# PSUM banks from a written list instead of from a pool, in a two-layer graph transformer

## The chip, the cores and the metric

One core of one Trainium2 chip runs the whole program in one launch. The metric is device time in microseconds (us); smaller is better. A core has five engines with a queue each: TensorE (PE in the profile, with its weight loads as PEld), VectorE (DVE), ScalarE (ACT), GpSimd (POOL) and SyncE (SP, which here only issues DMAs). Engines meet through semaphores: an instruction can wait until a counter that another engine raises has reached a value.

## The reference

32 graphs of 512 nodes with 256 features go through two attention layers. Everything is float32.

```python
x = _layernorm(x + _L0_gnn_ref(x, adj, ...), axis=-1)     # layer 0
x = _layernorm(x + _L1_gnn_ref(x, adj, ...), axis=-1)     # layer 1

def _L0_gnn_ref(x, adj, ...):            # 8 heads of 32
    allowed = (adj > 0) | (jnp.swapaxes(adj, 1, 2) > 0) | eye
    q, k, v = split(x @ Wqkv.T + bqkv)
    attn = softmax(where(allowed, q @ k.T / sqrt(32), -inf))
    x = _layernorm(x + (attn @ v) @ Wo.T + bo) * g1 + b1
    ff = relu(x @ W1.T + b1) @ W2.T + b2               # 256 -> 1024 -> 256
    return _layernorm(x + ff) * g2 + b2

def _L1_gnn_ref(x, adjacency, ...):      # no feed-forward part
    scores = where(adjacency == 0, -inf, q @ k.T / sqrt(32))
    return (softmax(scores) @ v) @ Wo.T + bo
```

So for each graph there are two attentions, one feed-forward block and four row normalisations (numbered 1 to 4 in the kernel: 1 after the first attention, 2 after the feed-forward part, 3 at the end of layer 0, 4 at the end of layer 1).

## The kernel before

The kernel keeps one graph's data in on-chip memory and is written as small steps, methods of a class `Graph`; one object stands for one of the 32 graphs. The order of the steps is written out by hand: `opening` starts the first graphs, `period(a, b, c, d, e)` (L1484) is called 26 times and moves five neighbouring graphs on by one stage each, and `closing` ends the last ones. In one `period`, graph `b` is in its second attention, graph `c` goes from the end of its first attention through its feed-forward block to the start of its second attention, and graph `d` starts its first attention. Each engine executes its own instructions strictly in the order in which the steps are listed.

PSUM, where TensorE writes its results, has eight banks[...]. Four banks hold the attention scores of one step (`s`), one holds the accumulated product of probabilities and values (`acc`), and the other three are the pool `ps_d` (L156), from which all other results of TensorE come: the dense products (`psQK`, `psV`, `psO`, `psH`, `psF`), the transpositions (`psT`), the row sums of the probabilities (`psR`) and some biases at the start (`psB`). Every such result is one tile, asked for in `bank` (L186). 1158 of them are made in the run. A bank that is used again makes the first matmul of the new tile wait until the last reader of the old tile in that bank is done, and until the old tile's own matmuls are.

The steps that matter below, with what they issue:

- `project(layer, h)` (L507): the output projection, psO, two blocks of 256 columns; read by DVE in `add(n, i)` (L515), n = 1 in layer 0 and 4 in layer 1, two adds for each psO tile (h = 0: i = 0 and 1; h = 1: i = 2 and 3).
- `transpose(n, h)` (L353): psT, four 128x128 transpositions; copied to SBUF by ACT in `transpose_out` (L363, L364).
- `hidden(h, f)` (L559): psH, two blocks of the hidden layer; read by ACT in `relu` (L567, L569). `mlp(i)` (L571) is the second product, psF, and `add(2, i)` reads it on DVE.
- `query_key(layer, which, c, h)` (L377): psQK; copied with its bias by ACT in `query_key_out` (L384, L388).
- `value(layer, h)` (L367): psV; copied by ACT in `value_out` (L374, L375).
- `scores` (L391), `exp` (L406, ACT, 2048 elements a row), `masked` (L409, DVE, L411), `product` (L413, L418) and `fold` (L433, DVE, L434) are the attention itself. They use no bank of `ps_d`.
- `sums` (L436, L442) is psR, read by DVE in `blocks` (L477, L483).
- `root` (L530, POOL), `offset` (L536, DVE, L538) and `norm` (L553, ACT, L554) normalise rows; `center` and `affine` (L542, L548, DVE) do so with gain and bias.

Dense products run through a helper, `dense` (L159), so all their matmuls have the line L162; the tile's name tells them apart. With `wide` off, a product is cut into four pieces of 32 output partitions that run side by side in TensorE.

Two places of `period` carry the prediction. The first is this one, graph `c` entering its feed-forward block (L1583 to L1603, other steps left out):

```python
c.add(1, 3)                      # DVE, reads psO
c.transpose(1, 0)                # PE
d.value(0, 1, wide=True)         # PE
c.transpose_out(1, 0)            # ACT
c.hidden(0, 4, wide=True)        # PE
c.hidden(0, 2, wide=True)        # PE
```

The second is graph `c` entering its second attention while `b` leaves it (L1737 to L1763):

```python
b.add(4, 2); c.query_key(1, 0, 0, 0); b.add(4, 1)
c.query_key_out(1, 0, 0, 0)      # ACT
d.product(0, 4); b.add(4, 3); d.product(0, 5)
c.value(1, 0)                    # PE
c.norm(3, 2); c.transpose(2, 1); b.add(4, 0)
c.query_key(1, 1, 0, 0, wide=True)
```

Of the kernel before, what the change touches and what calls it, by code (L numbers as in the profile page):

```python
# [9 lines left out]
F32 = mybir.dt.float32  # L10
# [17 lines left out]
def kernel(ctx: ExitStack, tc: tile.TileContext, t: dict, out: bass.AP):  # L28
# [15 lines left out]
    P = 128  # L44
# [106 lines left out]
    def plain(pools: ExitStack):  # L151
# [4 lines left out]
        ps_d = pools.enter_context(tc.tile_pool(name="ps_d", bufs=3, space=PSUM))  # L156
        hbm = pools.enter_context(tc.tile_pool(name="hbm", bufs=2, space=bass.MemoryType.DRAM))

        def dense(out, lhsT, rhs, start, stop, wide):  # L159
# [3 lines left out]

        SPREAD = {(0, 0), (1, 0)}

        SMALL = {"y", "z", "cent", "sT", "total", "r", "st", "part"} | {
            f"{t}{n}" for t in ("mv", "rs", "ms") for n in range(1, 5)
        }

        class Graph:  # L170
# [6 lines left out]
            def at(self, tag, n, shape, dtype=F32, **kw):  # L177

                key = (tag, n)
                if key not in self.tiles:  # L180
                    name = f"{tag}_{self.b}" + "".join(f"_{i}" for i in (n if isinstance(n, tuple) else () if n is None else (n,)))
                    pool = small if tag in SMALL else ps_s if tag == "s" else ps_a if tag == "acc" else work
                    self.tiles[key] = pool.tile([P, *shape], dtype, tag=tag, name=name, **kw)
                return self.tiles[key]

            def bank(self, kind, n, shape):  # L186

                key = (kind, n)
                if key not in self.tiles:
                    name = f"ps{kind}_{self.b}" + "".join(f"_{i}" for i in n)  # L190
                    self.tiles[key] = ps_d.tile([P, *shape], F32, tag="d", name=name)
                return self.tiles[key]

            def final(self, layer):
# [2497 lines left out]
    with ExitStack() as pools:  # L2692
        plain(pools)
# [207 lines left out]
```

## Time and profile before

| | us |
|---|---|
| median of 3 runs | 3055.63 |
| the 3 runs | 3054.47 to 3057.43 |
| the profiled execution, its device time | 3058.88 |
| its span, first to last instruction | 3057.1 |
| TensorE busy in the span | 2976.1 |
| VectorE busy | 2706.1 |
| ScalarE busy | 1746.1 |
| GpSimd busy | 921.5 |
| largest group on TensorE: scores, L398, 8192 passes | 573.6 |
| largest group on VectorE: masking, L411, 512 instructions of 2.278 us | 1162.4 |
| largest group on ScalarE: exp, L407, 512 instructions of 1.880 us | 962.8 |

The profile is one execution of the program. A matmul in it is a pipelined instruction: each stays in the record for 380 ns (256 columns) or 596 ns (512 columns), while the next one starts long before that; the end is modelled. A float32 product appears as two passes, a transposition as one. "Idle before" is the time for which an engine did nothing ahead of an instruction, with the engine and instruction that ended it, and gaps under 150 ns are not counted. The chain of waits follows the work that ended last back from the end of the program, at each step to what released it.

### The profile page before, as it was taken

What the parts mean: (1) busy time and instruction counts of PE and PEld (TensorE: products, weight loads), DVE (VectorE), ACT (ScalarE), POOL (GpSimd) and SP (SyncE); (2) the same over time, 40 slices, a digit from 0 to 9 for tenths busy, and PEclk for the clock granted to TensorE, in tenths of its full rate; (3) what the DMA queues carried; (4) which work ended last, traced back from release to release, by engine and by line L of the source; (5) the groups of instructions that cost most, each with busy time, mean ns of one, the idle gap of its engine ahead of it and who ended that gap; (6) DMA issues with size and microseconds to landing.
All of it is one profiled execution on the core that took longest, in us unless ns stands there. A gap on an engine that the chain in (4) does not pass through costs nothing.

```text
span 3057.1 us, 83051 instructions
## 1 busy us (share of the span) xinstructions
PE 2976.1 (97%) x36442; PEld 1374.6 (45%) x36442; DVE 2706.1 (89%) x3588; ACT 1746.1 (57%) x2111; POOL 921.5 (30%) x1252
## 2 busy tenths in 40 slices
PE   7989999999999999999999999999999999999997
PEld 2544444444444444444444444444444444444443
DVE  4879989989989999899899899998989998998996
ACT  4446655556555566565565555665655655556554
POOL 0222433323323223333233232333332333323231
PEclk9999999999999999999999999999999999999999
DMA  7657766666666676676666666766676666667551
GB/s 160 135 111 132 147 128 134 125 136 128 137 130 121 129 143 130 130 132 128 129 136 132 129 131 123 143 127 130 130 129 129 139 130 127 132 125 134 105 111 28
DMA packets 277169, 391.22 MB, mean 128 GB/s; under 512 B 153376, under 2 KB 237472, under 8 KB 246048
## 3 DMA queue, kind: packets, MB, share of 16 engines
q0 software_dynamic: 36304, 264.53, 47.5%
q1 hardware_dynamic: 240496, 121.32, 17.5%
q8 instruction: 288, 4.72, 0.6%
q14 instruction: 81, 0.66, 0.1%
HBM read 72.23 MB, written 33.55 MB: 35 GB/s over the span
## 4 chain that ended last, share of the span: by engine, by line
PE 77%; DVE 16%; issue 2%; POOL 2%; DMA 2%; ACT 1%; DVEq 0%; SPq 0%; POOLq 0%; ACTq 0%
PE psF L162 14%; PE psH L162 14%; PE s L398 13%; PE acc L418 10%; PE psQK_None L162 9%; DVE p L411 6%; PE psV L162 6%; PE psO L162 4%; PE psQK L162 3%; DVE p L434 3%; DVE st L525 2%; PE psR L442 2%; DVE y L522 2%; PE psT L359 1%; DMA p<-p 1%
## 5 line engine op out<-in xcount | busy, mean ns | idle before, releaser
L407 ACT ACTIVATE p<-s 128x2048 f32<-128x2048 f32 x512 | 962.8, 1880 | 502.6 <-PE s L398 468.8
L411 DVE TENSOR_TENSOR p<-p,m 128x2048 f32<-128x2048 f32 x512 | 1162.4, 2278 | 72.7 <-ACT p L407 72.6
L398 PE MATMUL s<-qT,kT 32*64 32x512 f32 x8192 | 573.6, 616 | 22.2 <-ACT p L407 20.9
L418 PE MATMUL acc<-p,v 128*32 128x512 f32 x4096 | 508.5, 596 | 1.7 <-ACT cT L427 1.5
L162 PE MATMUL psH<-xT,w_L_gnn_W 128*32 128x256 f32 (+1 forms) x6200 | 472.8, 380 | 16.5 <-DVE y L522 16.5
L162 PE MATMUL psF<-w_L_gnn_W,hT 128*32 128x256 f32 (+1 forms) x6704 | 462.2, 381 | 0.0
L434 DVE TENSOR_TENSOR p<-p,p 128x2048 f32<-128x2048 f32 x189 | 430.9, 2281 | 9.8 <-DMA p<-p 8.5
L533 POOL TENSOR_SCALAR rs<-mv 128x2 f32<-128x2 f32 (+1 forms) x320 | 189.1, 591 | 744.6 <-DVE mv L528 728.8
L162 PEld LDWEIGHTS psH<-xT,w_L_gnn_W 128*32 128x32 f32 (+1 forms) x6200 | 300.6, 119 | 222.0 <-issue 81.4
L162 PEld LDWEIGHTS psF<-w_L_gnn_W,hT 128*32 128x32 f32 (+1 forms) x6704 | 292.2, 116 | 180.5 <-ACT hT L569 33.1
L569 ACT ACTIVATE hT<-psH,c_L_gnn_b 128x256 f32<-128x256 f32 x512 | 211.3, 473 | 220.9 <-PE psH L162 220.9
L534 POOL TENSOR_TENSOR rs<-rs,neg_half 128x2 f32<-128x2 f32 (+1 forms) x320 | 327.1, 1022 | 26.7
L431 POOL DMA_DIRECT2D p<-p x189 | 174.2, 922 | 532.5 <-PE acc L418 468.8
L398 PEld LDWEIGHTS s<-qT,kT 32*64 32x64 f32 x8192 | 119.7, 130 | 335.6 <-issue 111.9
L162 PE MATMUL psQK_None<-xT,w_L_gnn_Wqkv 128*32 128x512 f32 (+1 forms) x2012 | 246.8, 596 | 5.9 <-DMA w_L_gnn_Wqkv<-in_L_gnn_Wqkv_dram 4.5
L162 PE MATMUL psO<-w_L_gnn_Wo,cT 128*32 128x256 f32 (+1 forms) x2776 | 241.8, 381 | 1.6 <-DVE cT L504 1.6
L458 POOL DMA_DIRECT2D p<-p x126 | 107.7, 855 | 440.3 <-DVE mv L528 196.2
L418 PEld LDWEIGHTS acc<-p,v 128*32 128x32 f32 x4096 | 119.7, 110 | 253.5 <-issue 188.5
L364 ACT COPY xT<-psT 128x512 f32<-128x512 f32 x130 | 76.0, 585 | 219.2 <-PE psT L359 219.1
L162 PEld LDWEIGHTS psO<-w_L_gnn_Wo,cT 128*32 128x32 f32 (+1 forms) x2776 | 155.3, 123 | 99.1 <-issue 45.4
L554 ACT ACTIVATE x<-z,ms,rs 128x256 f32<-128x256 f32 x128 | 73.0, 596 | 165.8 <-DVE ms L538 162.6
L525 DVE BATCH_NORM_STATS2 st<-y 128x6 f32<-128x256 f32 x384 | 154.9, 422 | 6.2
(77 smaller groups left out, 2845.4 us busy)
## 6 DMA issues: line engine op xcount, KB each, us to landing
p<-p POOLq DMA_DIRECT2D x189, 1024.0 KB, 7.8
p<-p POOLq DMA_DIRECT2D x63, 512.0 KB, 5.2
x<-in_x_dram SPq DMA_DIRECT2D x32, 512.0 KB, 4.2
code<-in_adj_dram POOLq DMA_DIRECT2D x32, 512.0 KB, 6.2
m<-code SPq DMA_DIRECT2D x32, 512.0 KB, 4.9
out_dram<-x SPq DMA_DIRECT2D x32, 512.0 KB, 4.7
p<-p POOLq DMA_DIRECT2D x63, 256.0 KB, 5.7
part<-p SPq DMA_DIRECT2D x252, 64.0 KB, 2.1
```

The costliest lines, as they stand in the source:

```text
L162: nc.tensor.matmul(out[at], lhsT[:, at], rhs, start=start, stop=stop)
L398: nc.tensor.matmul(s[half * P // 2 : (half + 1) * P // 2, j, :], self.kT(layer)[at, hg, key : key + P // 2], self.qT(layer)[at, hg, :], st ...
L407: nc.scalar.activation(self.p(layer, k), self.at("s", (layer, k), [HPC, N]), AF.Exp, scale=SCALE)
L411: nc.vector.tensor_tensor(p, p, m[:, k % NQ, None, :].to_broadcast([P, HPC, N]), ALU.mult)
L418: nc.tensor.matmul(acc[j * HD : (j + 1) * HD, :], self.v(layer)[:, kc, h * HD : (h + 1) * HD], self.p(layer, k)[:, j, :], start=(kc == 0), ...
L431: nc.gpsimd.dma_start(out=self.p(layer, k), in_=self.p(layer, k + 1), accum_op=ALU.add)
L434: nc.vector.tensor_tensor(self.p(layer, dst), self.p(layer, a), self.p(layer, b), ALU.add)
L458: nc.gpsimd.dma_start(out=p[:rows], in_=p[rows : 2 * rows], accum_op=ALU.add)
L525: nc.vector.bn_stats(self.at("st", (n, i), [6]), self.y(n, i))
L533: nc.gpsimd.tensor_scalar(rs, self.mv(n)[:, a:b, 1:2], EPS, None, ALU.add)
L534: nc.gpsimd.tensor_tensor(rs, rs, neg_half[:, a:b, None], ALU.pow)
L569: nc.scalar.activation(self.hT(h)[:, f, :], ps[:, f % 2, :], AF.Relu, bias=b1[:, f : f + 1])
```

## The change

`bank` gives each tile a tag of its own, `d0`, `d1` or `d2`, with one buffer for each tag, and takes the tag from a string of 1158 digits, one for each tile in the order in which the steps ask for them. Before, one tag had three buffers, and which of the three a tile got was settled when the program was put together.

```diff
+        banks = iter(
+            "012012021021122121012012010210210210201012102021121021012012012012102102102102102020120122021201212101120120212010"
+            + "120121212010121212012012120120021212102101010212101010210210102102201010" * 13
+            + "102120201210021021010210102102102021201021010210202101201201210210212102102102121021021021021021202102120120"
+        )
...
-                    self.tiles[key] = ps_d.tile([P, *shape], F32, tag="d", name=name)
+                    self.tiles[key] = ps_d.tile([P, *shape], F32, tag=f"d{next(banks)}", name=name, bufs=1)
```

There are still three banks for these tiles. The middle part of the string has 72 digits, for two calls of `period`, and is taken 13 times.

Put side by side, the two programs have the same instructions in the same order on every engine, and on DVE, ACT, POOL and SP the same waits. What differs is which tile had a tile's bank before it, for 138 of the 1158 tiles, and with it what 136 of TensorE's instructions wait for. 130 of the 138 are the same five tiles, once in each of the 26 turns:

| tile (graph) | bank held last by, before | and its reader | bank held last by, after | and its reader |
|---|---|---|---|---|
| `hidden(0, 4)` of c | `project(0, 1)` of c | DVE `add(1, 3)` | `transpose(1, 0)` of c | ACT `transpose_out(1, 0)` |
| `hidden(0, 2)` of c | `transpose(1, 0)` of c | ACT `transpose_out(1, 0)` | `project(0, 1)` of c | DVE `add(1, 3)` |
| `value(1, 0)` of c | `project(1, 1)` of b | DVE `add(4, 3)` | `query_key(1, 0, 0, 0)` of c | ACT `query_key_out(1, 0, 0, 0)` |
| `transpose(2, 1)` of c | `project(1, 0)` of b | DVE `add(4, 0)` | `project(1, 1)` of b | DVE `add(4, 3)` |
| `query_key(1, 1, 0, 0)` of c | `query_key(1, 0, 0, 0)` of c | ACT `query_key_out(1, 0, 0, 0)` | `project(1, 0)` of b | DVE `add(4, 0)` |

The other eight stand in `opening` (two) and `closing` (six). `hidden(0, 4)` also waits for `transpose_out(1, 0)` in both programs, because it multiplies what that step writes, and `transpose(2, 1)` waits for ACT's `norm(3, 2)` in both.

## The prediction

> **What bounds the kernel now.** I read the page's busy times first, then who waits for whom on TensorE, then one turn of the loop in order of time.
>
> ```profile
> PE 2976.1 (97%) x36442; PEld 1374.6 (45%) x36442; DVE 2706.1 (89%) x3588; ACT 1746.1 (57%) x2111; POOL 921.5 (30%) x1252
> ```
>
> TensorE is busy for 97% of the span, VectorE for 89%. TensorE's waits are few enough to be read one by one:
>
> ```profile
> PE s L398 <- ACT p L407: 20.9, 20, 8.5
> PE psH L162 <- DVE y L522: 16.5, 26, 0.6
> PE psV L162 <- DVE y L522: 14.9, 26, 0.6
> ```
>
> The columns are the total in us, how often, and the longest. The first row belongs to the start and the end of the run. The other two come 26 times each, once in each turn of the loop: psH starts at 365.19, 458.43, 551.65 and so on, every 93.22 us, until 2695.89; psV from 414.86 until 2745.55. Between 200 and 2746 us TensorE has no other gap of 150 ns. So each turn is TensorE's work plus these two stalls. What they are is seen in the turn around 1110 us (columns: start, duration, engine, line, operation, what it writes and reads, in brackets the idle time before):
>
> ```profile
> 1108.49 1.89 PE L162 MATMUL psV<-w_L_gnn_Wqkv,xT 128*128 128x256 f32 x8
> 1108.69 0.58 ACT L364 COPY xT<-psT 128x512 f32<-128x512 f32 x1 [2.14 <-PE psT L359]
> 1110.46 0.42 DVE L522 TENSOR_TENSOR y<-psO,x 128x256 f32<-128x256 f32 x1
> 1111.02 5.42 PE L162 MATMUL psH<-xT,w_L_gnn_W 128*128 128x256 f32 x24 [0.63 <-DVE y L522]
> ```
>
> The data of psH (xT) are there at 1109.27, when ACT's copy ends. psH starts only at 1111.02, because its bank was last psO's and DVE reads that until 1110.88. The chain of waits says why DVE is so late: the add stands behind two maskings of 2.2 us in its queue.
>
> ```profile
> 1106.14 4.40 DVE p L411 x2
> 1110.54 0.35 DVE y L522
> 1110.88 0.14 issue
> 1111.02 5.42 PE psH L162 x24
> ```
>
> The second stall, 50 us later in the same turn:
>
> ```profile
> 1158.20 1.90 PE L418 MATMUL acc<-p,v 128*32 128x512 f32 x16
> 1159.26 0.47 ACT L388 ACTIVATE qT<-psQK,c_L_gnn_bq 128x256 f32<-128x256 f32 x1
> 1160.21 0.41 DVE L522 TENSOR_TENSOR y<-psO,x 128x256 f32<-128x256 f32 x1
> 1160.67 1.94 PE L162 MATMUL psV<-w_L_gnn_Wv,xT 128*32 128x256 f32 x32 [0.57 <-DVE y L522]
> 1161.11 0.60 ACT L554 ACTIVATE x<-z,ms,rs 128x256 f32<-128x256 f32 x1 [0.57 <-DVE ms L538]
> 1161.15 0.39 DVE L522 TENSOR_TENSOR y<-psO,x 128x256 f32<-128x256 f32 x1
> 1162.54 0.66 PE L359 MATMUL psT<-ident,x 128*128 128x128 f32 x4
> ```
>
> psV waits for the add that ends at 1160.62; psQK's reader on ACT was done at 1159.73.
>
> **What the Trainium skill says.** "Perfetto Trace Analysis", section "Optimization Strategy": a gap that repeats on the engine that should be saturated can mean that there is no buffer for the next tile. The trace agrees: 26 equal gaps of each kind, on tiles whose inputs are ready. "PSUM — Partial Sum Buffer", section "PSUM bank collisions raise a hardware error": engines must be kept apart by semaphores by bank, not by address; so whoever takes a bank waits for its last reader, as psH does here for a tile that it never reads. The same page, "Engine vs sequencer instructions": VectorE's and ScalarE's queues are strictly in order; hence the add behind two maskings. "TensorE: Matmul & The Clock Gate", section "What's actually happening": the default clock is the throttled one and activity releases it. Here the loop runs at a granted 1.00, the first 365 us at 0.96.
>
> **The change part by part.** No instruction is added, removed or moved, and only TensorE's waits differ. I take each stall's price from starts, since the modelled ends hide a part of it.
>
> *hidden(0, 4).* Passes of 256 columns follow each other every (1.89 − 0.38)/7 = 0.216 us in the psV row (0.38 is one pass). The last psV pass thus starts at 1110.00 and psH is due at 1110.22; it comes at 1111.02, 0.80 late. Its 24 passes then take 5.42 − 0.38 = 5.04 us from first to last start where 23 × 0.216 = 4.97 would do: 0.07 more, because the weight loads had not run ahead. Sum 0.87. After the change it waits for ACT's copy alone, done 0.95 us before 1110.22. Gain 0.87.
>
> *hidden(0, 2)* gets the wait for the add. It is due eight passes after 1110.22, at 1111.95; the add is done at 1110.88, as it does not depend on the stall. Cost 0, with 1.07 us of cover. Were DVE later than that, each us would cost a us; behind it stand the other psH tiles and their relus on ACT.
>
> *value(1, 0).* Four pieces side by side take 0.43 us per 512 columns (TensorE's weight loads for acc come in groups of four at 1104.70, 1105.13, 1105.56), so the 16 passes of acc end their starts 4 × 0.43 after 1158.20 and psV is due at 1159.92. It comes at 1160.67: 0.75. Its 32 passes, eight groups of 0.216, should take 1.73; psT comes 1.87 later: 0.14. Sum 0.89. After, psV waits for ACT's qT copy, which ends at 1159.73, before 1159.92. Behind psV on TensorE stand transpose(2, 1), three psQK and the scores on which ACT's next exp depends.
>
> *transpose(2, 1)* would then be due at 1161.65. It needs ACT's norm(3, 2), which ends at 1161.71 and hangs on a chain over DVE and POOL that starts with the end of psF at 1151.3, not with the stall. From ACT's end to a dependent matmul I take 0.07 us (the psQK row at 1163.89 follows an ACT copy that ends at 1163.82). So psT starts at 1161.78, 0.76 earlier than 1162.54, and 0.13 of the 0.89 stay. Its new bank's reader, the third add, ends at 1160.62. *query_key(1, 1, 0, 0)* now waits for the fourth add, done at 1161.54; it is due 0.49 after psT, at 1162.27. Cover 0.73, cost 0.
>
> *The tiles in opening and closing:* each new wait there ended at least 0.3 us before its matmul started anyway. 0.
>
> Sum per turn 0.87 + 0.76 = 1.63; 26 × 1.63 = 42.4 us. All other waits of the new program are met at the times of the old trace, so with the same durations nothing can be late.
>
> **What is late next.** DVE, which has 84.6 us of work in a turn that will take 91.6, and two places where it waited for TensorE just long enough:
>
> ```profile
> 1133.75 0.72 DVE L483 STREAM_TRANSPOSE sT<-psR 128x512 f32<-128x512 f32 x1 [0.92 <-PE psR L442]
> 1173.55 2.29 DVE L411 TENSOR_TENSOR p<-p,m 128x2048 f32<-128x2048 f32 x1 [0.91 <-ACT p L407]
> ```
>
> From the add after the second psO (1101.62) to psR at 1133.75 DVE never waits for TensorE, so a TensorE that is 0.87 early there uses 0.87 of the 0.92; the second place gives 0.76 of its 0.91. Both just suffice, and 1.28 us more (before the add after psF, 1151.32) lie behind the first. DMA landings are 3 us or more ahead of the compute instructions that need them.
>
> **The rivals.** (A) Only one stall pays: DVE or the chain to norm(3, 2) holds the second place. For it: the norm already takes 0.13 there. Against: that chain starts at psF, which moves with the first gain. 26 × 0.87 = 22.6, so 3033.0. (B) All is given back in the same turn, because DVE's queue becomes the bound. For it: 89% busy, margins of 0.05 and 0.15. Against: it has 8.6 us free in a turn. 3055.6. (C) Slower: the denser matmuls cost clock. Place: the whole loop. At the opening's 0.96, the 92.0 us of TensorE's work in a turn take 3.8 more, less 1.63: 26 × 2.2 = 57, so 3113; it decides from 1.63/92.0, a grant under 0.982. Against: the loop has 1.00 where TensorE is busiest, and the page's activity rule points the other way. (D) The list repeats the old choice: excluded, since 136 waits differ.
>
> **How the numbers follow.** The profiled execution's 3058.88 (span 3057.1 and 1.8 around it) lies 3.25 above the median of 3055.63, so I take the 42.4 from the median: 3013.2. Bounds: if norm(3, 2) costs nothing, 26 × 1.76 = 45.8, 3009.8; if DVE's margins hold back 0.3 us in a turn, 3021. The likeliest case has 0.80 (3008 to 3021), A 0.10, B 0.06, C 0.04. The range takes in A and a little below the lower bound: 3007 to 3034. Measurements of this kernel tell 0.2% (6 us) from no change. Faster 0.80 + 0.10 + part of B: 0.92; same 0.05; slower 0.03.
>
> **What would show it.** In the profile after: the rows psH and psV waiting for DVE y gone; turns of 91.6 us; TensorE busy for some 11 us less (the tails of 0.24 and 0.19 us that a stall adds to the modelled busy time), at 98% of a span near 3015; DVE's wait for psR down from 0.92 to under 0.1 and for exp from 0.91 to about 0.15; psT's weights waiting for ACT x. Wrong if a new wait of TensorE comes 26 times, or the granted clock falls.

## The result, and the profile after

| | before, us | after, us |
|---|---|---|
| median | 3056.2 (3054.47 to 3057.43, 4 runs) | 3014.36 (3012.29 to 3019.34, 4 runs) |
| profiled execution | 3058.88 | 3012.29 |
| its span | 3057.1 | 3010.5 |

The ratio is 0.9866 (95% interval 0.9849 to 0.9883): 1.3% faster, 41.8 us between the medians, where 42.4 were forecast. The lines of `bank` and all that follows are six lines further down in the kernel after: L411 before is L417 now.

First the page, its busy times and its chain of waits:

```profile
PE 2959.1 (98%) x36442; PEld 1375.9 (46%) x36442; DVE 2707.0 (90%) x3588; ACT 1746.2 (58%) x2111; POOL 972.2 (32%) x1252
...
PE 93%; DVE 3%; DMA 2%; ACT 1%; issue 1%; POOL 1%; SPq 0%; DVEq 0%; POOLq 0%; ACTq 0%
```

The same instructions are executed. The chain that ended last has become TensorE's almost alone: 93% of the span, against 77% before, when DVE had 16% of it. That share of DVE was its queue ahead of the two adds. The list of who waits for whom, TensorE alone, its largest entries (total in us, times, longest):

```profile
PE s L404 <- ACT p L413: 21.4, 19, 8.5
PE psT L365 <- DMA x<-in_x_dram: 4.9, 1, 4.9
PE psQK_None L162 <- DMA w_L_gnn_Wqkv<-in_L_gnn_Wqkv_dram: 4.7, 1, 4.7
PE ps_total L2871 <- DVE total_row L2869: 3.3, 1, 3.3
```

Both rows with 26 entries are gone and none has come in their place; what is left belongs to the start and the end of the run. One turn of the loop, from one transpose(1, 0) to the next, in windows of the two kernels (start and end, length, busy time of PE, PEld, DVE, ACT, POOL with their instructions, granted clock, DMA share, GB/s); before first:

```profile
1108.00:1201.23 93.23, 92.03 (x1125) 42.85 (x1117) 84.67 (x113) 54.55 (x66) 29.18 (x39) 1.00 0.66 131
```

```profile
1092.86:1184.44 91.58, 91.58 (x1125) 43.02 (x1117) 84.71 (x113) 54.55 (x66) 31.18 (x39) 1.00 0.69 133
```

The turn lasts 91.58 us instead of 93.23, and TensorE is busy in all of it. DVE's work in a turn is the same 84.7 us. The first place, in order of time, in the kernel after:

```profile
1093.35 1.89 PE L162 MATMUL psV<-w_L_gnn_Wqkv,xT 128*128 128x256 f32 x8
1093.55 0.59 ACT L370 COPY xT<-psT 128x512 f32<-128x512 f32 x1 [2.14 <-PE psT L365]
1095.08 5.34 PE L162 MATMUL psH<-xT,w_L_gnn_W 128*128 128x256 f32 x24
1095.31 0.42 DVE L528 TENSOR_TENSOR y<-psO,x 128x256 f32<-128x256 f32 x1
```

psH starts 1.73 us after psV, which is eight passes of 0.216 and no stall, and it starts before the add that it used to wait for. The 24 passes take 5.34 us instead of 5.42, so the loss of 0.07 at the restart is gone too. The second place:

```profile
1142.19 1.90 PE L424 MATMUL acc<-p,v 128*32 128x512 f32 x16
...
1143.25 0.47 ACT L394 ACTIVATE qT<-psQK,c_L_gnn_bq 128x256 f32<-128x256 f32 x1
...
1143.77 1.56 PEld L162 LDWEIGHTS psV<-w_L_gnn_Wv,xT 128*32 128x32 f32 x32 [0.59 <-ACT qT L394]
...
1143.90 1.91 PE L162 MATMUL psV<-w_L_gnn_Wv,xT 128*32 128x256 f32 x32
...
1145.10 0.60 ACT L560 ACTIVATE x<-z,ms,rs 128x256 f32<-128x256 f32 x1 [0.57 <-DVE ms L544]
...
1145.75 0.66 PE L365 MATMUL psT<-ident,x 128*128 128x128 f32 x4
```

psV starts 1.71 us after acc, its due time. Its weights wait for ACT's qT copy, as the new list has it, and are released 0.13 us before the first matmul starts, at its due time: no cost. psT starts 0.05 us after ACT's norm ends, so it looks as if it were held by it, as forecast; one of the experiments asks whether it is.

### The profile page after: what moved, and what is told of

It reads as the page before. It is cut to its first block, busy times and chain, and to the rows that moved or that the text cites. A ratio compares the mean times of both kernels' runs of the same rounds, so it can differ in the third digit from the quotient of the medians.

```text
span 3010.5 us, 82999 instructions
## 1 busy us (share of the span) xinstructions
PE 2959.1 (98%) x36442; PEld 1375.9 (46%) x36442; DVE 2707.0 (90%) x3588; ACT 1746.2 (58%) x2111; POOL 972.2 (32%) x1252
## 4 chain that ended last, share of the span: by engine, by line
PE 93%; DVE 3%; DMA 2%; ACT 1%; issue 1%; POOL 1%; SPq 0%; DVEq 0%; POOLq 0%; ACTq 0%
PE s L404 17%; PE psF L162 14%; PE acc L424 14%; PE psH L162 14%; PE psQK_None L162 11%; PE psV L162 7%; PE psO L162 7%; PE psQK L162 4%; PE psT L365 2%; PE psR L448 2%; DMA p<-p 1%; DVE p L417 1%; ACT p L413 1%; DVE p L440 1%; DMA w_L_gnn_Wqkv<-in_L_gnn_Wqkv_dram 0%
## 5 line engine op out<-in xcount | busy, mean ns | idle before, releaser
L417 DVE TENSOR_TENSOR p<-p,m 128x2048 f32<-128x2048 f32 x512 | 1162.5, 2278 | 49.9 <-ACT p L413 46.7
L539 POOL TENSOR_SCALAR rs<-mv 128x2 f32<-128x2 f32 (+1 forms) x320 | 196.5, 614 | 726.6 <-DVE mv L534 713.3
L540 POOL TENSOR_TENSOR rs<-rs,neg_half 128x2 f32<-128x2 f32 (+1 forms) x320 | 369.7, 1155 | 26.7
```

Of the source, the lines that this page charges most:

```text
L417: nc.vector.tensor_tensor(p, p, m[:, k % NQ, None, :].to_broadcast([P, HPC, N]), ALU.mult)
L539: nc.gpsimd.tensor_scalar(rs, self.mv(n)[:, a:b, 1:2], EPS, None, ALU.add)
L540: nc.gpsimd.tensor_tensor(rs, rs, neg_half[:, a:b, None], ALU.pow)
```

## The experiments

All times are medians. The first five rows are from one chip, the last four from another.

| kernel | us | ratio to before (95%) |
|---|---|---|
| before, beside the first four | 3057.0 (9 runs) | |
| the change once more | 3014.58 (3014.28 to 3014.79) | 0.9861 (0.9845 to 0.9876) |
| new banks at the first place only | 3034.02 (3032.58 to 3035.32) | 0.9924 (0.9911 to 0.9938) |
| new banks at the second place only | 3038.68 (3037.95 to 3039.2) | 0.9939 (0.9926 to 0.9953) |
| the change, root ahead of halve | 3012.81 (3011.99 to 3013.98) | 0.9854 (0.9838 to 0.987) |
| before, beside the last three | 3056.38 (11 runs) | |
| the change, one more DVE instruction | 3013.27 (3010.34 to 3014.5) | 0.9859 (0.9843 to 0.9874) |
| the change, six more | 3065.45 (3061.27 to 3067.13) | 1.0029 (1.0017 to 1.004) |
| the change, 17 matmuls in an idle time | 3017.16 (3013.04 to 3025.45) | 0.9884 (0.9868 to 0.9899) |

The second row is the yardstick: the median of the change comes again to 0.2 us. In all the profiles I took the same four legs of a turn from the starts of TensorE's instructions, averaged over the 26 turns (in us):

| leg | before | after | first place only | second only |
|---|---|---|---|---|
| transpose(1, 0) to hidden(0, 2) | 4.821 | 3.948 | 3.948 | 4.819 |
| hidden(0, 2) to query_key(1, 0, 0, 0) | 44.493 | 44.493 | 44.493 | 44.494 |
| query_key(1, 0, 0, 0) to transpose(2, 1) | 5.227 | 4.450 | 5.227 | 4.453 |
| transpose(2, 1) to the next transpose(1, 0) | 38.687 | 38.687 | 38.686 | 38.686 |

**One place at a time.** The lists of these two kernels were made from the old choice of banks, with the tiles of one place exchanged. The digits of one turn's tiles from transpose(1, 0) on, named so that bank 0 is the one used last before them:

```diff
 the first place only
-2012121201201212012021
+2021212102102121021012
 the second place only
-2012121201201212012021
+2012121201201212012002
```

(In the upper pair the third and fourth digit are hidden(0, 4) and hidden(0, 2); what follows is renamed with them. In the lower pair the last two are value(1, 0) and transpose(2, 1).)

> The new banks for hidden(0, 4) and hidden(0, 2) alone, in all 26 turns; value(1, 0), transpose(2, 1), query_key(1, 1, 0, 0) and the tiles of opening and closing keep the tile before them that they had. Theory (each stall is a wait for a bank and has its own price): 26 x 0.87 = 22.6 us less than before, about 3033.5; the row psV waiting for DVE y stays with 26 x 0.57, psH is gone. Rival (the two gains lean on each other, the second place being held by DVE unless the first is free, or the other way round): one of the two single versions gives nothing, the other all 42. Rival (the gain comes from opening and closing): no change here.

Measured: 3034.02, 23.0 less than before. In its list of waits the second place stands as it was:

```profile
PE psV L162 <- DVE y L537: 15.0, 26, 0.6
```

> The new banks for value(1, 0), transpose(2, 1) and query_key(1, 1, 0, 0) alone, in all 26 turns. Theory: 26 x 0.77 = 20 us less than before, about 3036; the row psH waiting for DVE y stays with 26 x 0.63, psV is gone. Rival (DVE holds the second place when the first stall is still there): no change, 3056. If the sum of both single gains is that of the change (42 to 43 us), the stalls are independent.

Measured: 3038.68, 18.3 less than the median of before, and 20.2 less if the two profiled executions are set side by side (3038.68 and 3058.88). The first place stands:

```profile
PE psH L162 <- DVE y L537: 16.5, 26, 0.6
```

The leg of the place that was changed takes its new length to within 0.003 us, and the other three don't move. Neither place needs the other. The gains of the medians add up to 41.3, against 42.4 for both together on that chip. The rivals that tie the two together, or that put the gain outside the turns, fall. So does the thought that taking banks from a list, with one buffer for each tag, is faster in itself: both of these kernels have such a list, and each keeps the stall whose banks it left as they were.

**What holds transpose(2, 1).** One step of POOL goes ahead of a DMA that POOL issues:

```diff
+            c.root(3, 2, 3)
             d.halve(0, 0, P // 2)
             ...
-            c.root(3, 2, 3)
             c.offset(3, 2, 3)
```

> The changed kernel with one POOL step moved: root(3, 2, 3) ahead of the accumulating DMA halve(0, 0, P // 2), so that norm(3, 2) on ACT, which transpose(2, 1) needs, is done about 0.4 us earlier. Theory (after the change transpose(2, 1) is held by norm(3, 2), by the 0.11 us that are left of the second stall): 26 x 0.11 = 3 us less than the changed kernel, about 3011.5, and query_key to transpose(2, 1) falls from 4.45 to 4.33 us. Rival (the 0.11 us are TensorE's own change of tiling): no change, 3014.4. Rival (the halved sums come later by 1.3 us and DVE waits for them): slower than the changed kernel, DVE shows an idle time at L489.

Measured: 3012.81. The place in its order of time:

```profile
1145.67 1.91 PE L162 MATMUL psV<-w_L_gnn_Wv,xT 128*32 128x256 f32 x32
1145.69 0.60 ACT L560 ACTIVATE x<-z,ms,rs 128x256 f32<-128x256 f32 x1 [0.20 <-DVE ms L544]
...
1146.47 0.60 ACT L560 ACTIVATE x<-z,ms,rs 128x256 f32<-128x256 f32 x1 [0.19 <-DVE ms L544]
...
1147.51 0.42 PEld L365 LDWEIGHTS psT<-ident,x 128*128 128x128 f32 x4 [0.41 <-ACT x L560]
1147.51 0.66 PE L365 MATMUL psT<-ident,x 128*128 128x128 f32 x4
```

The norm is now done at 1147.08, 0.43 us before psT instead of 0.05. Yet psT starts 1.84 us after psV, where it was 1.85, and the leg shrinks from 4.454 (in the repeated change) to 4.445, the same in all 26 turns. So norm(3, 2) cost 0.01 us, not 0.11. The profile still names ACT's x as what released psT's weights, which is why such an entry alone doesn't prove a wait.

The rest is TensorE's own. It goes here from products in four pieces of 32 columns to a transposition over all 128, and from the last pass of the one to the first pass of the other it takes 0.31 us: in this kernel, where nothing is waited for, and in the kernel before as well. Other places of the turn point to the change of shape. In the trace of the change, 192 times between 400 and 2600 us a last pass of 256 columns is followed by scores, which have yet another shape: 0.31 us each time, after four pieces as after all 128. Where four pieces are followed by four pieces (168 times), it is 0.20.

The time is 1.8 us below that of the repeated change, but 0.01 × 26 is 0.3, and its profiled execution (3013.98) differs from that of the repeated change (3014.53) by 0.55. The rest of the 1.8 is not explained by the edit; the scatter of the clock described at the end is of this size. It is not claimed as a faster version.

**How much room DVE has.** `stats(1, 3)` is issued twice, or seven times, in each turn:

```diff
             c.stats(1, 3)
+            c.stats(1, 3)
```

> The changed kernel with one more VectorE instruction in each turn: stats(1, 3) twice, 0.42 us, between the add that hidden(0, 2) waits for and the row sums (the result is the same, the second writes what the first wrote). Theory (TensorE alone sets the turn, VectorE has slack): no change, 3014.6; VectorE's idle time behind the row sums takes it. Rival B of the prediction (after the change VectorE is the bound, its margin of 0.05 us used up): 26 x 0.42 = 11 us more, 3025.5.

Measured: 3013.27, no cost. After the change DVE has used up just the margins that were named. Here are its instructions at the two spots, in the kernel after:

```profile
1117.20 0.48 DVE L550 SCALAR_TENSOR_TENSOR cent<-y,mv,s_L_gnn_ln_g 128x256 f32<-128x256 f32 x1
1117.73 0.72 DVE L489 STREAM_TRANSPOSE sT<-psR 128x512 f32<-128x512 f32 x1
```

```profile
1156.45 0.17 DVE L544 SCALAR_TENSOR_TENSOR ms<-mv,rs 128x2 f32<-128x2 f32 x1
1156.77 2.29 DVE L417 TENSOR_TENSOR p<-p,m 128x2048 f32<-128x2048 f32 x1
```

0.05 us are left ahead of the row sums (0.92 before) and 0.15 ahead of the masking (0.91). But a late DVE there makes nobody wait at once, and the added instruction is absorbed further on: transpose(1, 1) on TensorE, which needs DVE's affine(1, 2), starts 0.57 us after that has ended, instead of 1.03.

> The same with six more, 2.5 us in each turn, to see where VectorE's slack ends. Theory: transpose(1, 1) on TensorE waits for affine(1, 2) and had 1.90 us of slack before the change, 1.03 after; so TensorE stalls 1.5 us there in each turn and the time is 26 x 1.5 = 39 us more than the changed kernel, about 3053. Rival B (VectorE is the bound already): all of it shows, 26 x 2.5 = 65 us more, 3080. A third (VectorE has slack of over 2.5 us): no change.

Measured: 3065.45, 50.9 more than the change (as it ran on the first chip), where the theory had 39 and rival B 65. The place is the one the theory named:

```profile
PE psT L365 <- DVE x L557: 44.9, 26, 1.7
```

The size was off by three terms. The seven instructions take 3.20 us instead of 0.43, so 2.77 were added and not 2.5. Of the 1.03 us of slack only 0.97 can be used: 0.06 lie between the end of DVE's instruction and the transposition even when TensorE stands waiting for it. 2.77 − 0.97 = 1.80, and by 1.80 us 23 of the 26 turns are longer. The other three are longer by 3.48: in them 3.41 us at a granted clock of 0.50 follow upon TensorE's stop (from 661.02, 1036.49 and 1971.74 us on), and half of that is lost. On average the turn is 93.58, 2.00 longer, and 26 × 2.00 = 52. So TensorE bounds the turn, and DVE has about 1 us of room ahead of transpose(1, 1), no more.

**Outside the turns.** 26 times the saving of the legs, 0.873 + 0.777, is 42.9 us, but the span fell by 46.6. The other 3.7 lie before the first turn (1.95) and after the last (1.75). The changed banks there are not the cause. The change itself, once more, needed 362.28 us ahead of its first turn, as much as the kernel before (362.17), where its first profile had 360.22; and after the last turn the kernel with the first place alone, which has the old banks there, is shorter too, by 1.56. The windows of the granted clock say what it is. Before, and below it the change, at the same place in the program (scores(0, 4) of graph 30, behind an idle time of TensorE of 2.62 and 2.51 us):

```profile
2802.10:2804.00 1.90, 1.90 (x20) 0.43 (x24) 1.90 (x1) 1.69 (x5) 0.00 (x0) 0.64 0.61 95
2804.00:2806.00 2.00, 2.00 (x24) 0.98 (x20) 0.75 (x2) 2.00 (x2) 0.00 (x0) 0.50 1.03 359
```

```profile
2757.10:2759.00 1.90, 1.86 (x32) 0.79 (x36) 1.89 (x1) 1.90 (x5) 0.00 (x0) 1.00 0.74 141
2759.00:2761.00 2.00, 2.00 (x44) 1.18 (x36) 1.07 (x2) 1.78 (x2) 0.00 (x0) 1.00 1.00 346
```

The third figure from the end is the clock: half in one execution, full in the other. What such a stretch costs can be read in the opening, where every execution has one around scores(0, 1). From the start of scores(0, 1) to the first turn the nine profiles take 168.11 to 169.17 us, of which 3.17 to 5.31 us are at half clock. When half of that time is taken off, 166.51 to 166.53 us are left in eight of them and 166.62 in the ninth, the kernel with 17 matmuls below. So each us at half clock costs half a us there. Of the 1.95, 1.01 arose here, and the rest ahead of it.

I tried to get such a stretch out of the way, in the longest idle time of the opening, with matmuls whose results nobody reads:

```diff
+            b.warm(17)
             c.scores(0, 1)
...
+            def warm(self, count):
+                ps = self.bank("T", (1, 1), [ND, 2 * P])
+                for _ in range(count):
+                    nc.tensor.matmul(ps[:, 0, :], ident, w1[:, 0, : 2 * P], start=True, stop=True)
```

> The changed kernel with 17 matmuls more in the opening, in the one long idle time of TensorE there (8.5 us ahead of scores(0, 1) at 193.7 us); they write a bank that transpose(1, 1) overwrites later and their results are not used. It tests what made 1.75 and 1.95 us of difference outside the turns: stretches of 3.41 us and multiples at a granted clock of 0.5 that follow an idle TensorE. Theory: the stretch of 10.24 us at 0.5 from 187.6 on is gone, the 4.2 us of work that fell into it take 2.1 less, 3012.5; the turns stay at 91.58. Rival (ScalarE's exp bounds the place, the clock doesn't matter): 3014.6. Rival (the added matmuls delay the scores): slower, with the idle time before scores gone.

Measured: 3017.16, from 3013.04 to 3025.45, so nothing is gained. The windows at the place, the repeated change and then this kernel:

```profile
188.00:192.00 4.00, 0.00 (x0) 0.00 (x0) 0.00 (x0) 0.27 (x1) 0.00 (x0) 0.50 0.92 198
192.00:196.00 4.00, 2.34 (x18) 0.73 (x19) 2.36 (x2) 2.31 (x3) 0.00 (x0) 0.50 0.91 138
```

```profile
188.00:192.00 4.00, 1.31 (x19) 0.34 (x17) 0.83 (x1) 2.35 (x2) 0.00 (x0) 1.00 0.82 123
192.00:196.00 4.00, 4.00 (x20) 3.14 (x13) 3.47 (x3) 2.35 (x2) 0.00 (x0) 0.59 0.30 68
```

The half clock is later and shorter (3.41 us instead of 10.24), but it isn't gone: 2.69 us of idle time were left ahead of scores(0, 1), and all 3.41 us fall into work, where 4.17 of the 10.24 did. From there to the first turn this takes 0.29 us less, not 2.1. That scores(0, 1) starts 2.5 us earlier comes from ahead of the added matmuls: TensorE's work before them ends at 180.97 us instead of 184.90, with 10.24 us at half clock so far instead of 17.07. The turns are the same 91.58, and another stretch of half clock stands after the last turn of this execution. So the place of the stretch moved with the idle time; that the run can be made shorter in this way is not shown. The profile is of the fastest of its four runs, and their spread is left open.

## Why the prediction was right

- *The sum.* The legs saved 1.650 us in a turn where 1.63 were forecast; that is the forecast that was tested. That the medians agree to 0.6 us as well is in part luck, as the opening and the closing each differ by 2 us and more between executions.
- *The bound.* TensorE with two stalls in each turn: shown. Both rows vanished, and the two other legs of the turn stayed within 0.001 us.
- *hidden(0, 4).* 0.87 forecast, 0.873 measured, alone and together with the other. Reckoning from starts was needed: the idle time in the profile is 0.63, since the last matmul's modelled end covers 0.16 of the gap, and 0.07 are lost after the restart, which no idle time shows.
- *hidden(0, 2)* with the wait for the add, *query_key(1, 1, 0, 0)* with the wait for the fourth add: no cost, as forecast. Neither appears among TensorE's waits.
- *value(1, 0)* started on time.
- *transpose(2, 1).* The gain of 0.76 was met (0.777), but by a wrong account. The prediction counted 0.14 us after psV as a part of the stall's 0.89. Of these, 0.11 are the change of shape on TensorE, which stays, stall or not; only 0.02 went with the stall, whose price was thus 0.78. The prediction then put about as much as it had counted too high, 0.13, down to norm(3, 2), and so the two errors cancelled, which is luck. The kernel with the earlier norm showed that the norm holds 0.01. The lower bound of 3009.8 "if norm(3, 2) costs nothing" was thus not to be had.
- *DVE's margins.* 0.05 and 0.15 us forecast, 0.05 and 0.15 in the trace after. Its idle time before psR's readers fell from 39.0 to 14.4 us (26 × 0.87 = 22.6 was to go).
- *Busy time of TensorE.* 17.0 us less, not 11. In the turns it is 11.5, as forecast. The rest lies outside them, which the forecast didn't treat: 3.9 us before the first turn (0.8 when the change was run again) and the others after the last, where the stretches at half clock differ.
- *The rivals.* One stall only (A): the single kernels give each its own gain. DVE as the bound (B): one more instruction costs nothing. Clock (C): 1.00 in all turns of the kernel after. Why the result could not be on the slower side with equal durations was said in the prediction: all new waits were met at the old times.

## What to carry to other kernels

When a pool of PSUM banks is shared by tiles with different readers, look at each repeated gap of TensorE and ask whose tile was in the bank before: the wait is for that tile's reader, and for all that stands ahead of it in its queue. Give a bank back first to a tile that waits for the same reader anyway, here psH for the ACT copy that writes its own input, and leave a slow reader's bank for the next tile. Price such a stall by the starts of the matmuls around it, and take from a place without a wait what two products of these shapes need anyway. Then check each wait that is added against the old trace; where all are met with time to spare, the gain is the stall.

## What the runs showed of the hardware

The granted clock was 1.00 or 0.50, nothing between, in the clock records of all these traces, and the stretches at 0.50, the end of the program apart, lasted 3.41 us or two to five times that: before the first turn of the kernel before 3.41, 13.65 and 10.24. The Trainium skill, "TensorE: Matmul & The Clock Gate", section "What's actually happening", has a free-running window of 3413 ns and these two states; the traces agree.

The length of a short idle time of TensorE did not settle whether such a stretch followed. At the place after the last turn, idle times of 2.62, 2.64 and 2.61 us (before, second place only, the one with 17 matmuls) had 3.41 us at half clock beside them, and 2.68 us in another execution (first place only) had none; nor had 2.46 to 2.51 us in the five others. With six more DVE instructions, TensorE stood still for 1.73 us in each of the 26 turns, and three times a stretch of 3.41 us followed. Each us at half clock cost half a us of the run where TensorE was the bound: in the opening, and in the three turns just named, which took 1.69 us longer than the other 23. From the last turn's transpose(2, 1) to the end the three executions with a stretch took 309.5 to 309.7 us and the six without 307.6 to 308.1, whichever banks their tiles had there.
